# Which products of queries and keys GpSimd makes in an eight-layer sequence: three of seventeen in place of two

## The chip, the cores and the metric

The kernel runs on 1 core of one Trainium2 chip. The metric is the device time of one execution in microseconds. The engines are named as the profile names them: PE is TensorE, DVE is VectorE, ACT is ScalarE, POOL is GpSimd, and SP is SyncE, which issues the DMAs here. ("PEld" is the loading of weights into PE.)

## The reference

Four blocks of a network, each an attention-like layer and a feed-forward layer, eight layers in all, over 4 sequences of 1024 tokens with 128 features. Each layer's output is added to its input and normalised:

```python
x = L0_attn_data
x = _layernorm(x + _L0_attn_ref(x, ...), axis=-1)
x = _layernorm(x + _L0_ffn_ref(x, ...), axis=-1)
x = _layernorm(x + _L1_attn_ref(x, ...), axis=-1)
x = _layernorm(x + _L1_ffn_ref(x, ...), axis=-1)
...
```

The change lies in the third layer, an attention inside each token: every one of 16 heads has 64 scalar queries, keys and values, and the scores are all products of a query with a key up to its own index.

```python
def _L1_attn_ref(x, Wq, bq, Wk, bk, Wv, bv, Wo, bo):
    H, C = (16, 64)
    Q = (x @ Wq + bq).reshape(b, s, H, C) * inv_sqrt_c
    K = (x @ Wk + bk).reshape(b, s, H, C)
    V = (x @ Wv + bv).reshape(b, s, H, C)
    scores = jnp.einsum('bshq,bshk->bshqk', Q, K)
    mask = jnp.triu(jnp.ones((C, C), dtype=bool), 1)
    scores = jnp.where(mask, jnp.asarray(-jnp.inf, scores.dtype), scores)
    w = jax.nn.softmax(scores, axis=-1)
    attn = jnp.einsum('bshqk,bshk->bshq', w, V)
    return attn.reshape(b, s, HID) @ Wo + bo
```

So there are 4096 tokens x 16 heads x 64 queries, each against up to 64 keys, and no matrix product makes the scores: they are elementwise products.

## The kernel before

**Units.** The 4096 tokens are 32 tiles of 128, and each tile is two units of 64 tokens: 64 units. In a unit the 128 partitions are 32 tokens times 4 of the keys (key index modulo 4), and the free dimension runs over 2 lots of 32 tokens, 16 heads and the queries. The 64 keys of a head are thus 16 groups (n = 0 to 15) of 4. With a group n only the queries from 4(n + 1) on meet all its keys, so the product with "n" has 64 - 4(n + 1) queries per head (60 for n = 0, 4 for n = 14), that is 32 times as many columns. The queries on the diagonal are two more products, "d", with 32 queries per head (1024 columns) each. That makes seventeen products a unit, fed in this order (`feed`, lines 850 to 894): d1, n8 to n14, d0, n0 to n7.

**One product's way.** Each of the seventeen takes room in a ring of 8904 columns (`ringe` in the profile) and goes through the engines in turn (`rest`, from line 903 on):

1. product of queries and keys into the ring, by DVE, which reads the keys where they lie in PSUM (`ringe<-qr,kvr`), or, for the products that `SHARED` names, by POOL;
2. subtraction of the row's maximum in place, always by POOL (`ringe<-ringe,mr`);
3. exponential in place, by ACT;
4. sum over partitions into the denominators, by PE (`den`);
5. multiplication by the values in PSUM, in place, by DVE (`ringe<-ringe,kvr`);
6. sum over partitions into the numerators, by PE (`num`), after which the room in the ring is free.

Denominators, values and numerators run strictly in the order of the products. POOL can't take the keys from PSUM, so for each shared product ACT first copies the 32 keys per partition into a small tile (`ks`, in `keys_values`, lines 839 to 842).

```python
shared = (kind, i) in SHARED
yield "POOL" if shared else "DVE", self.when(
    lambda: self.ering.can(SH * nq), lambda: self.ering.back(SH * nq)
), True
...
if shared:
    self.g.tensor_tensor(e, qk[0], unit["ks"][i][:, :, None].to_broadcast(sh), ALU.mult)
else:
    self.v.tensor_tensor(e, *qk, ALU.mult)
```

**Around it.** `prepare` makes queries and the row maxima of a tile ahead (two scans, a predicated copy and a product on DVE per half), copies them with DMAs on SP's queue into `qr` and `mr`, two buffers each, and `keys_values` makes keys and values of a unit on PE into two PSUM buffers (`kvr`). `close` divides and projects a finished unit. Three further chains follow the attention through the later layers, group by group of 512 tokens (the last 512 in two groups of 256): chain a (the ternary feed-forward layer, a recurrence, an expert layer), chain b (a state space layer) and chain c (a routed layer, whose tables POOL gathers by indirect DMA: `gt<-in_f_tup`, `gt<-in_f_tdn`).

**The order.** All instructions are written out in one order per engine by a planner in the kernel (`Order`): it keeps a clock for each engine from formulas for the length of every operation (`length`), and at each step takes the task that can start first. Among tasks of one engine that could start within 0.05 us of each other it takes the most urgent kind: closing a unit, then preparing, then the three chains, then the steps 2 to 6 ("rest"), and last the products ("feed"). The feed is one sequence: the product after one on POOL is placed only when that one has been placed. At run time each engine works through its list in order and waits by semaphores.

Every operation is recorded through a helper, so all lines of the profile carry its line 60 (L60); groups are told apart by their tiles.

Of the kernel before, what the change touches and what calls it, by code (L numbers as in the profile page):

```python
# [309 lines left out]
class Model:  # L310
# [511 lines left out]
    def keys_values(self, unit, u, xt):  # L822

        for half in (1, 0):
# [13 lines left out]
            yield "ACT"  # L838
            for kind, n in SHARED:
                if n // 8 == half:  # L840
# [7 lines left out]
    def feed(self):  # L848
# [6 lines left out]
        for unit in self.units:  # L855
            seen = set()
            for kind, i in order:
# [14 lines left out]
                else:  # L872
# [5 lines left out]
                    shape = lambda tt, nq=nq: tt.rearrange("p (a q) -> p a q", q=nq)  # L878
                shared = (kind, i) in SHARED
                yield "POOL" if shared else "DVE", self.when(  # L880
# [1033 lines left out]
            self.order.run()  # L1914
        assert not self.held and all(len(self.slots[k]) >= n for k, (n, _) in self.room.items()), self.slots

SHARED = ("n", 8), ("n", 3)

URGE = {"close": 0, "prepare": 1, "chain_a": 2, "chain_b": 2, "chain_c": 2, "rest": 3, "feed": 4}
HOP = {"close": 0.2, "prepare": 0.2, "chain_a": 0.5, "chain_b": 0.5, "chain_c": 0.5, "rest": 0.1, "feed": 0.1}  # L1920
# [122 lines left out]
```

## Time and profile before

| | us |
|---|---|
| median of 3 runs | 3988.96 |
| lowest and highest run | 3988.85, 3995.15 |
| profiled execution | 3998.63 |
| its span, first to last instruction | 3996.9 |

The mean clock that PE was granted is 0.909 of full speed. Attention's products run from 88.8 us (the first on POOL) to about 3590 us; the rest of the span is the end of the three chains. The groups of the profile that belong to the steps above:

| step | engine | instructions | busy us |
|---|---|---|---|
| product | DVE | 960 | 1106.0 |
| product | POOL | 128 | 287.3 |
| subtraction | POOL | 1088 | 2549.8 |
| exponential, n | ACT | 962 (a few of other work) | 998.4 |
| exponential, d | ACT | 512 | 353.4 |
| denominators | PE | 8710 | 688.4 |
| values | DVE | 1102 (a few of other work) | 1291.3 |
| numerators | PE | 8712 | 697.7 |
| copies of keys | ACT | 128 | 22.6 |

960 + 128 products and 1088 subtractions are 64 units of seventeen. How to read the views: a group's row gives line, engine, operation, output tile <- input tiles, shapes and count, then busy time and the mean duration of one in ns, then the idle time of the engine just before them and what ended it. A row of waits gives who waited for whom, us in total, how often, and the longest.

### The profile page before, as it was taken

The numbers are of one execution on the slowest core, as the hardware profiler recorded it, in microseconds if no ns is written. First come the engines' busy times: TensorE is split into PE (matmuls) and PEld (weight loads), VectorE is DVE, ScalarE is ACT, GpSimd is POOL, SyncE is SP. The second block draws the span as 40 slices with busy tenths as digits, with TensorE's granted clock in tenths as the row PEclk, the third lists the DMA queues.
The fourth block names the chain that finished last, engine by engine and source line by source line (L and its number), as shares of the span: only waits on it lengthen the run. The fifth ranks groups of instructions, "written<-read, shape, count | busy, mean of one in ns | idle before, by whom it ended". The sixth has DMA issues, their size and how long they took to land.

```text
span 3996.9 us, 94513 instructions
## 1 busy us (share of the span) xinstructions
PE 3255.3 (81%) x38498; PEld 1703.2 (43%) x38498; DVE 3263.9 (82%) x4477; ACT 2613.7 (65%) x4970; POOL 2914.4 (73%) x1320
## 2 busy tenths in 40 slices
PE   6677677777898887888898988988898887879873
PEld 3242233333344443444354454444344443447552
DVE  3879898998988899999988889899988889983421
ACT  5675575567677786677567876677666785656441
POOL 1879996899688889698778777698787887880000
PEclk8897888888999999999899999999899998999896
DMA  3211221212223233343233234243332334522564
GB/s 86 63 46 44 56 63 44 56 43 49 57 68 93 58 93 93 76 114 88 74 95 80 70 83 105 66 128 78 96 90 63 87 80 117 148 76 70 149 147 103
DMA packets 385164, 329.13 MB, mean 82 GB/s; under 512 B 196108, under 2 KB 320460, under 8 KB 384728
## 3 DMA queue, kind: packets, MB, share of 16 engines
q1 hardware_dynamic: 375384, 289.53, 29.4%
q0 software_dynamic: 9344, 33.56, 2.8%
q8 instruction: 302, 4.95, 0.5%
q14 instruction: 134, 1.10, 0.1%
HBM read 147.85 MB, written 40.89 MB: 47 GB/s over the span
## 4 chain that ended last, share of the span: by engine, by line
PE 23%; DVE 16%; ACT 9%; issue 8%; POOL 7%; DMA 5%; SPq 1%; DVEq 0%; POOLq 0%; ACTq 0%
PE bg L60 13%; DVE ringe L60 10%; POOL ringe L60 7%; PE num L60 4%; PE den L60 4%; ACT ringe L60 4%; DVE bg L60 3%; PE kvr L60 2%; ACT b L60 1%; SPq L60 1%; ACT ha L60 1%; ACT L60 1%; DVE b L60 0%; DMA mr<-td 0%; DMA td<-gt 0%
## 5 line engine op out<-in xcount | busy, mean ns | idle before, releaser
L60 POOL TENSOR_TENSOR ringe<-ringe,mr 128x1024 f32<-128x1024 f32 (+14 forms) x1088 | 2549.8, 2378 | 524.9 <-DVE ringe L60 370.9
L60 DVE TENSOR_TENSOR ringe<-ringe,kvr 128x1024 f32<-128x1024 f32 (+14 forms) x1102 | 1291.3, 1204 | 171.0 <-PE den L60 148.4
L60 ACT ACTIVATE ringe<-ringe 128x896 f32<-128x896 f32 (+14 forms) x962 | 998.4, 1055 | 585.0 <-POOL ringe L60 582.8
L60 DVE TENSOR_TENSOR ringe<-qr,kvr 128x1024 f32<-128x1024 f32 (+12 forms) x960 | 1106.0, 1188 | 61.9 <-PE num L60 47.5
L60 PE MATMUL num<-ringe,cst 128*32 128x256 f32 (+7 forms) x8712 | 697.7, 412 | 242.6 <-DVE ringe L60 237.9
L60 PE MATMUL den<-ringe,cst 128*32 128x256 f32 (+7 forms) x8710 | 688.4, 417 | 201.7 <-ACT ringe L60 162.0
L60 PEld LDWEIGHTS num<-ringe,cst 128*32 128x32 f32 x8712 | 206.3, 113 | 589.4 <-DVE ringe L60 450.5
L60 PEld LDWEIGHTS den<-ringe,cst 128*32 128x32 f32 x8710 | 226.5, 114 | 517.8 <-ACT ringe L60 256.1
L60 ACT ACTIVATE ringe<-ringe,cst 128x256 f32<-128x256 f32 x512 | 353.4, 772 | 61.7 <-POOL ringe L60 61.2
L60 POOL TENSOR_TENSOR ringe<-qr,ks 128x896 f32<-128x896 f32 (+1 forms) x128 | 287.3, 2245 | 82.4 <-PE num L60 44.4
L60 PE MATMUL bg<-xT,a 128*128 128x512 f32 (+2 forms) x486 | 254.5, 636 | 15.4 <-DVE a L60 4.9
L60 PE MATMUL bg<-a,ha 128*128 128x128 f32 x1168 | 165.8, 288 | 14.3 <-ACT ha L60 14.3
L60 DVE TENSOR_TENSOR_SCAN bg<-ends,bg 128x512 f32<-128x512 bf16 x128 | 155.3, 1218 | 25.5 <-PE bg L60 23.9
L60 PE MATMUL kvr<-wkv,xT 128*32 128x256 f32 x2048 | 153.5, 423 | 24.3 <-DVE ringe L60 23.8
L60 PEld LDWEIGHTS bg<-a,ha 128*128 128x128 f32 x1168 | 147.5, 198 | 23.7 <-ACT ha L60 15.7
L60 POOL DMA_INDIRECT gt<-in_f_tup,dlumps x16 | 15.8, 987 | 185.4 <-ACT dlumps L60 136.5
L60 ACT COPY b<-bg 128x256 f32<-128x256 f32 (+2 forms) x216 | 96.3, 450 | 69.2 <-PE bg L60 67.0
L60 PE MATMUL bg<-xT,b 128*128 128x128 f32 (+1 forms) x884 | 133.8, 295 | 9.4 <-DVE b L60 2.8
L60 ACT ACTIVATE ha<-bg,cst 128x512 f32<-128x512 f32 (+1 forms) x150 | 98.2, 675 | 62.4 <-PE bg L60 62.1
L60 PEld LDWEIGHTS bg<-xT,a 128*128 128x128 f32 (+1 forms) x486 | 85.7, 201 | 118.9 <-issue 59.2
L60 PEld LDWEIGHTS bg<-xT,b 128*128 128x128 f32 x884 | 112.6, 198 | 48.1 <-issue 23.3
L60 ACT ACTIVATE b<-cst,little 128x128 f32<-128x128 f32 x392 | 125.0, 396 | 0.0
(653 smaller groups left out, 4652.3 us busy)
## 6 DMA issues: line engine op xcount, KB each, us to landing
qr<-q SPq DMA_DIRECT2D x512, 128.0 KB
mr<-t SPq DMA_DIRECT2D x512, 128.0 KB
a<-in_f_W SPq DMA_DIRECT2D x67, 256.0 KB
c<-in_f_Wdn SPq DMA_DIRECT2D x58, 256.0 KB
c<-tu SPq DMA_DIRECT2D x212, 64.0 KB
tu<-gt SPq DMA_DIRECT2D x26, 512.0 KB
td<-gt SPq DMA_DIRECT2D x24, 512.0 KB
c<-td SPq DMA_DIRECT2D x88, 128.0 KB
```

The source lines that it names most:

```text
L60: return f(*args, **kw)
```

## The change

`SHARED` names the products that POOL makes. Before: n8 (28 queries per head, 896 columns) and n3 (48 queries, 1536 columns), 76 queries in all. After: n10 (20 queries, 640 columns), n1 (56 queries, 1792 columns) and n5 (40 queries, 1280 columns), 116 in all. The products n8 and n3 are then made by DVE from the keys in PSUM. ACT copies three sets of keys in place of two: one in the half with n8 to n15, two in the other. The places of POOL's products among the seventeen are the 2nd and 13th before, and the 4th, 11th and 15th after.

```diff
@@ -1914,7 +1914,7 @@
-SHARED = ("n", 8), ("n", 3)
+SHARED = ("n", 10), ("n", 1), ("n", 5)
```

Nothing else differs in the text; the planner derives the order of all engines anew from it.

## The prediction

> **What bounds the kernel now.** I read the summary of engines first, then the busy time by stretch, then the groups by shape, then the waits, and last cut the stretch of attention into slices of 10 us.
>
> The busy times, with the share of the span, and the head of the chain that ended last:
>
> ```profile
> PE 3255.3 (81%) x38498; PEld 1703.2 (43%) x38498; DVE 3263.9 (82%) x4477; ACT 2613.7 (65%) x4970; POOL 2914.4 (73%) x1320
> ...
> PE 23%; DVE 16%; ACT 9%; issue 8%; POOL 7%; DMA 5%; SPq 1%; DVEq 0%; POOLq 0%; ACTq 0%
> ```
>
> No engine is full and the chain passes over all of them (as far back as it can be followed, to about 1260 us), so no single total decides. By stretch (length, then busy us and instructions of PE, weight loads, DVE, ACT and POOL, then clock and DMA):
>
> ```profile
> 100.00:3600.00 3500.00, 2905.06 (x33732) 1452.80 (x33733) 3117.43 (x4032) 2388.90 (x4316) 2880.51 (x1279) 0.92 0.31 78
> 3600.00:3997.00 397.00, 287.85 (x4537) 214.40 (x4535) 113.06 (x369) 171.10 (x521) 22.74 (x25) 0.84 0.47 117
> ...
> 400.00:600.00 200.00, 141.24 (x1449) 54.15 (x1450) 180.91 (x188) 129.82 (x180) 194.34 (x86) 0.83 0.25 59
> ...
> 1800.00:2000.00 200.00, 170.93 (x2239) 85.40 (x2243) 184.16 (x234) 135.53 (x232) 156.32 (x67) 0.92 0.32 82
> ```
>
> The changed work ends at about 3600 us; the last 397 us hold none of it. In the 3500 us before, DVE is 89.1% busy (3117.43 / 3500) and POOL 82.3%. POOL is at 97% from 400 to 600 us, DVE ahead of it at 92% to 78% from 1800 to 2000: the bound changes hands. The waits (us in total, times, longest):
>
> ```profile
> ACT ringe L60 <- POOL ringe L60: 644.0, 434, 7.2
> ...
> POOL ringe L60 <- DVE ringe L60: 378.5, 115, 34.0
> ...
> DVE ringe L60 <- PE den L60: 157.9, 136, 8.9
> ```
>
> POOL waits for products of DVE (378.5 us): DVE is late there. The exponentials wait for subtractions of POOL (644.0 us), and DVE waits for denominators, which stand behind those exponentials: POOL is late there. To weigh the two I counted, over 350 slices of 10 us from 100 to 3600 us, which engine was busy over 95%. Two such slices:
>
> ```profile
> 400.00:410.00 10.00, 8.23 (x72) 2.06 (x72) 6.95 (x6) 5.32 (x6) 10.00 (x5) 0.70 0.57 127
> 1470.00:1480.00 10.00, 7.75 (x142) 4.02 (x144) 9.89 (x17) 9.87 (x24) 6.74 (x4) 1.00 0.16 52
> ```
>
> The first counts for POOL alone, the second for DVE alone. The count: DVE alone 112 slices, POOL alone 104, both 70, neither but PE 29, none of the three 35. Up to 1000 us it is POOL 39 to DVE 20, from 1000 to 2000 us 22 to 39, from 2000 us on 43 to 53.
>
> **The change part by part.** A unit has 544 query columns per head over its seventeen products, so 17,408 columns; 64 units run. The rows for the sizes concerned (busy us, mean ns of one; then idle time):
>
> ```profile
> L60 POOL TENSOR_TENSOR ringe<-qr,ks 128x1536 f32<-128x1536 f32 x64 | 177.5, 2773 | 55.2 <-PE num L60 44.4 <-DVE ringe L60 7.7 <-ACT anm L60 2.6
> ...
> L60 POOL TENSOR_TENSOR ringe<-qr,ks 128x896 f32<-128x896 f32 x64 | 109.8, 1716 | 27.2 <-ACT ks L60 22.3 <-ACT b L60 3.4 <-DMA qr<-q 1.2
> ...
> L60 DVE TENSOR_TENSOR ringe<-qr,kvr 128x1792 f32<-128x1792 f32 x64 | 128.8, 2012 | 5.3 <-PE num L60 5.3
> ...
> L60 DVE TENSOR_TENSOR ringe<-ringe,kvr 128x1536 f32<-128x1536 f32 x64 | 111.8, 1747 | 24.0 <-PE den L60 21.9 <-ACT xT L60 2.0
> ...
> L60 DVE TENSOR_TENSOR ringe<-qr,kvr 128x1280 f32<-128x1280 f32 x64 | 94.7, 1480 | 4.4 <-PE num L60 4.3
> ...
> L60 DVE TENSOR_TENSOR ringe<-ringe,kvr 128x896 f32<-128x896 f32 x64 | 69.2, 1081 | 5.6 <-PE den L60 5.5 <-issue 0.2
> ...
> L60 DVE TENSOR_TENSOR ringe<-qr,kvr 128x640 f32<-128x640 f32 x64 | 52.2, 816 | 0.0
> ```
>
> DVE loses the products of 1792, 1280 and 640 columns: 2012 + 1480 + 816 = 4308 ns a unit. It gets back those of 1536 and 896 columns. Their rows on DVE don't exist as products; the multiplication by the values has the same shape and one operand in PSUM too, and where both rows exist they agree (1215 and 1215 ns at 1024 columns), so 1747 + 1081 = 2828 ns. DVE is relieved of 1.48 us a unit, 94.7 us in all.
>
> POOL loses 2773 + 1716 = 4489 ns a unit. Its products at 640, 1280 and 1792 columns aren't in the trace. A line through its two rows has 1.652 ns a column ((2773 - 1716) / 640) and 236 ns fixed: 1293 + 2350 + 3196 = 6839 ns, so 2.35 us more a unit, 150.4 us in all. The bounds are the two rows taken as plain rates for 3712 columns: 1.805 ns gives 6701 (2.21 us more), 1.915 ns gives 7109 (2.62 us more). I take the line: 1280 columns lie between its points, and 640 and 1792 lie 256 columns outside on either side, so that an error of its slope nearly cancels.
>
> The Trainium skill ("GPSIMD Engine Reference", section 3.1) measures GpSimd 1.96 times slower than VectorE on two-input elementwise work and keeps VectorE as the rule. Here the ratio is smaller, 1716 / 1081 = 1.59. By the page the three products would take 1.96 x 4308 = 8444 ns and the addition would be an estimated 3.96 us a unit, which makes the sum below +80 us in place of +29. The skill ("Perfetto Trace Analysis", "Optimizing Scalar/DVE Operations") also warns that the two engines share a port, so that moving work between them may not help. No such blocking shows: DVE's products run from 270 to 2158 ns over all sizes while its largest size has a mean of 2147 ns, with POOL busy 82% of the time.
>
> ACT makes three copies of keys (176 ns each) in place of two: 64 x 0.176 = 11.3 us. It is 68% busy (2388.90 / 3500), and two of the three now stand back to back behind one wait, so I cost this at nothing; uncovered it is 11.3 us. No transfer is added. The products still read the landed queries and hold the same ring space.
>
> The moved product stands in POOL's queue with the subtractions and the gathers of the last layer. It takes its place in the order in which products are fed, so nothing behind it in that order is fed first: POOL has three such points in a unit, after which DVE's next products follow. What is late behind a product on POOL is a subtraction, then its exponential on ACT, then denominators on PE, then DVE's multiplication by values. A gather can be late by at most one product (3.2 us, where it was 2.8); those after 3600 us meet none.
>
> **The sum.** POOL's work on a unit is (2549.8 + 287.3) / 64 = 44.33 us, and grows by 2.35 us, 5.3%. DVE is busy 3117.43 / 64 = 48.7 us a unit, and falls by 1.48 us, 3.0%. Where POOL alone is full, time follows POOL: 1040 us x 5.3% = +55. Where DVE alone is full: 1120 us x 3.0% = -34. Where both are full I take half of each, since either can be last: 700 us x 1.15% = +8. Where neither is full: nothing. Sum: +29 us. With the bounds of POOL's price (5.0 to 5.9%) it is +25 to +36.
>
> The profiled execution took 3998.63 us for a span of 3996.9, so the sum gives a span of 4026. This execution stands 9.7 us above the median of the runs, 3988.96; from that median the forecast is 4018 us, and the times below start from it too.
>
> **The rivals.**
>
> *DVE sets the pace (faster).* POOL is idle 620 of the 3500 us, 378.5 of them waiting for DVE. If the added 2.35 us falls into that idle time, only DVE's relief counts: -34 us where DVE alone is full, -55 with the slices where both are (1820 us x 3.0%); 3934 to 3955 us, and 3944 in the middle. For it: DVE is the busier engine, and the ring's 8904 columns hold half a unit, so that POOL can work off its backlog. Against it: the gain needs DVE-full time 1.75 times the POOL-full time (5.3 / 3.04), and it is 112 to 104. Its place is the start of a unit, where POOL waits for the first product; it decides if POOL's backlog never reaches the exponentials.
>
> *Neither engine decides (same).* PE is 83% busy and has the largest share of the chain; the gains and losses cancel within 8 us: 3981 to 3997 us. For it: 64 slices with neither of the two full. Against it: 286 with one of them or both.
>
> *POOL becomes the bound (much slower).* If the slices where both are full go POOL's way and DVE's relief is worth nothing, (1040 + 700) x 5.3% = +92 us, 4081 us; if every unit pays, +150 us, 4139 us. For it: after the change POOL carries 3031 us (2880.51 + 150.4) and DVE 3023 in the same stretch. Against it: POOL's idle time must take none of it.
>
> That the change does something else than it says is excluded: the list of shared products is read in two places only, for the copies and for the engine.
>
> **How the numbers follow.** A measurement here tells no less than about 0.2% (8 us) from no change. Forecast, slower by 8 to 92 us (3997 to 4081): 0.48. Beyond it, POOL as the bound: 0.06. Same: 0.10. Faster: 0.36, of which 0.07 beyond 3940 us, since every later decision of the order moves with the first and that can add to either side. So slower 0.54, same 0.10, faster 0.36. The range 3940 to 4080 leaves out 0.07 below and about 0.06 above; the likeliest case has 3997 to 4081.
>
> **What would show it.** POOL's three products at 1.29, 2.35 and 3.2 us and DVE's busy time down by 95 us would confirm the prices; POOL's busy time should rise to about 3065 us. The theory is right if the slices with POOL alone full grow at DVE's cost, if exponentials wait longer for POOL than 644 us, and if the first 1000 us, where POOL leads 39 to 20, lose most (+17 by the same sum: 390 x 5.3% - 200 x 3.0% + 200 x 1.15%). It is wrong if POOL's wait for DVE falls from 378.5 us by more than 100 us while the end of attention comes earlier than 3600 us: then the idle time took the work. It is wrong too if the time changes mostly after attention, in the last 397 us.

## The result, and the profile after

The changed kernel takes 4003.56 us (median of 9 runs, 3997.64 to 4012.14); before, on the same chips, 3990.8 us (9 runs, 3988.85 to 3998.6). The ratio is 1.0029, 95% interval 1.0017 to 1.0041: slower by 7 to 16 us, where +29 was forecast. The two profiled executions hide this: the one of before lies 7.8 us above its median and the one of after 2.5 us below, so that their spans, 3996.9 and 3999.3 us, differ by only 2.4 us. The traces are read below for where work moved, and the medians for what it cost.

The summary of engines after, and the head of the chain:

```profile
PE 3237.4 (81%) x38498; PEld 1690.0 (42%) x38498; DVE 3181.3 (80%) x4413; ACT 2612.4 (65%) x5034; POOL 3060.1 (77%) x1384
...
PE 34%; DVE 24%; POOL 15%; ACT 14%; issue 9%; DMA 3%; SPq 1%; DVEq 0%; POOLq 0%; ACTq 0%
```

The two stretches after (length, then busy us and instructions of PE, weight loads, DVE, ACT and POOL, then clock and DMA):

```profile
100.00:3600.00 3500.00, 2888.20 (x33609) 1435.02 (x33601) 3022.15 (x3932) 2386.37 (x4365) 3024.49 (x1341) 0.93 0.31 77
3600.00:3999.00 399.00, 287.30 (x4661) 220.32 (x4660) 128.71 (x408) 171.51 (x533) 25.59 (x28) 0.84 0.50 129
```

POOL rose from 2880.51 to 3024.49 us and DVE fell from 3117.43 to 3022.15: the two are level. The products after, by shape, on POOL and then on DVE (busy us, mean ns; idle time before them):

```profile
L60 POOL TENSOR_TENSOR ringe<-qr,ks 128x1792 f32<-128x1792 f32 x64 | 205.0, 3203 | 9.1 <-PE num L60 9.0
...
L60 POOL TENSOR_TENSOR ringe<-qr,ks 128x1280 f32<-128x1280 f32 x64 | 150.2, 2346 | 8.2 <-PE num L60 7.3 <-DVE bg L60 0.8
...
L60 POOL TENSOR_TENSOR ringe<-qr,ks 128x640 f32<-128x640 f32 x64 | 81.6, 1276 | 0.5 <-PE num L60 0.5
```

```profile
L60 DVE TENSOR_TENSOR ringe<-qr,kvr 128x1536 f32<-128x1536 f32 x64 | 111.6, 1744 | 13.2 <-PE num L60 13.1
...
L60 DVE TENSOR_TENSOR ringe<-qr,kvr 128x896 f32<-128x896 f32 x64 | 68.9, 1076 | 0.0
```

The prices of single instructions were right to within 2% (forecast 3196, 2350, 1293, 1747 and 1081 ns). The waits after (us, times, longest):

```profile
ACT ringe L60 <- POOL ringe L60: 670.6, 442, 11.0
...
POOL ringe L60 <- DVE ringe L60: 327.8, 79, 24.1
...
DVE ringe L60 <- PE den L60: 224.7, 154, 9.2
```

POOL waits less for DVE (378.5 us before), the exponentials wait a little more for POOL, and DVE, which has less to do, waits more for the denominators behind those exponentials (157.9 before). The count of 10 us slices turned the same way: POOL alone full 153 (104 before), DVE alone 83 (112), both 62 (70).

When a unit ends can be read from one instruction: the division that closes it. In order of time, the division of unit 32 in the traces of before and of after (start, length):

```profile
1786.46 0.69 DVE L60 TENSOR_TENSOR rd<-num,rd 128x512 f32<-128x512 f32 x1
```

```profile
1834.38 0.68 DVE L60 TENSOR_TENSOR rd<-num,rd 128x512 f32<-128x512 f32 x1
```

By the 32nd unit of 64 the changed kernel is 48 us late; at the 64th it is 7 us late. This shape, a loss in the first half and a gain in the second, was the first question for the experiments. The ends of units (us):

| profiled kernel | unit 16 | unit 32 | unit 48 | unit 64 | span |
|---|---|---|---|---|---|
| before | 918 | 1787 | 2709 | 3603 | 3996.9 |
| after | 949 | 1835 | 2731 | 3610 | 3999.3 |
| pair, then three | 916 | 1786 | 2701 | 3585 | 3987.3 |
| three, then pair | 949 | 1833 | 2735 | 3616 | 4015.4 |
| more on POOL, old order | 940 | 1829 | 2776 | 3702 | 4094.2 |
| less on DVE, old order | 911 | 1776 | 2696 | 3585 | 3981.1 |
| more on POOL, own order | 942 | 1844 | 2766 | 3660 | 4036.0 |
| less on DVE, own order | 912 | 1777 | 2651 | 3547 | 3940.8 |

### The profile page after: what moved, and what is told of

It is laid out like the page before. It is cut to its first block, busy times and chain, and to the rows that moved or that the text cites. A ratio compares the mean times of both kernels' runs of the same rounds, so it can differ in the third digit from the quotient of the medians.

```text
span 3999.3 us, 94470 instructions
## 1 busy us (share of the span) xinstructions
PE 3237.4 (81%) x38498; PEld 1690.0 (42%) x38498; DVE 3181.3 (80%) x4413; ACT 2612.4 (65%) x5034; POOL 3060.1 (77%) x1384
## 4 chain that ended last, share of the span: by engine, by line
PE 34%; DVE 24%; POOL 15%; ACT 14%; issue 9%; DMA 3%; SPq 1%; DVEq 0%; POOLq 0%; ACTq 0%
PE bg L60 19%; DVE ringe L60 16%; POOL ringe L60 14%; PE den L60 6%; ACT ringe L60 6%; PE num L60 6%; DVE bg L60 5%; PE kvr L60 3%; ACT ha L60 1%; ACT b L60 1%; ACT L60 1%; DVE a L60 1%; ACT bg L60 1%; ACT x L60 1%; SPq L60 1%
## 5 line engine op out<-in xcount | busy, mean ns | idle before, releaser
L60 ACT ACTIVATE ringe<-ringe 128x640 f32<-128x640 f32 (+14 forms) x964 | 998.5, 1056 | 602.0 <-POOL ringe L60 598.1
L60 DVE TENSOR_TENSOR ringe<-qr,kvr 128x1024 f32<-128x1024 f32 (+11 forms) x896 | 1011.1, 1163 | 59.9 <-PE num L60 45.0
L60 POOL TENSOR_TENSOR ringe<-qr,ks 128x640 f32<-128x640 f32 (+2 forms) x192 | 436.8, 2275 | 17.9 <-PE num L60 16.8
L60 ACT COPY b<-bg 128x512 f32<-128x512 f32 (+2 forms) x229 | 101.8, 453 | 85.4 <-PE bg L60 82.8
L60 PE MATMUL bg<-b,cst 128*128 128x512 f32 x208 | 116.6, 644 | 6.8 <-ACT b L60 5.1
```

The source lines that it names most:

```text
L60: return f(*args, **kw)
```

## The experiments

Each was timed beside the kernel before on its chip; ratios are to that, with their 95% interval. "The pair" is n8 and n3, "the three" are n10, n1 and n5.

**Halves.** The obvious reading of the table's first two rows is that POOL sets the pace of the first half and DVE that of the second. Two kernels share by the number of the unit:

```diff
-                shared = (kind, i) in SHARED
+                shared = (kind, i) in shared_of(2 * unit["T"] + unit["u"])
...
+def shared_of(k):
+    return PAIR if k < 32 else THREE
```

The copies of keys use the same function; the second kernel has the two exchanged.

> The first 32 units share as before (n8, n3), the last 32 as after (n10, n1, n5). Theory A (POOL sets the pace of the first half, where every unit pays for POOL's added 2.35 us; DVE sets it in the second half, where its relief of 1.48 us a unit comes through): unit 32 ends as before (1787 us), the second half is some 40 us shorter, and the whole takes 3945 to 3965 us against 3991, faster by 0.7 to 1.2%. Rival B (the second half of the changed kernel only catches up work of the later layers that was put off in the first half, with no gain of its own): 3985 to 4000 us. Rival C (the end hangs on the later layers, not on attention): attention ends some 40 us earlier but the whole gains less than 10 us.

> The first 32 units share as after (n10, n1, n5), the last 32 as before. Theory A: unit 32 ends 40 to 48 us later than before and nothing is got back: 4030 to 4040 us. Rival B (catching up of put-off work): the second half wins the time back with the old pair too, 3990 to 4010 us.

Measured: 3990.82 us, 0.9991 (0.9982 to 1.0000), and 4017.59 us, 1.0061 (1.0047 to 1.0074). Theory A falls: with the three in the second half alone the gain is some 4 us and not 40. Rival B is right about the first kernel and misses the second, which took more than its 3990 to 4010 us and less than theory A's 4030 to 4040. With the pair in the second half the time won back is still large: 46 us late at unit 32, 13 at unit 64. So most of this recovery needed no relief of DVE. The later layers show what could have been exchanged. The state space layer clears its state before its third group; the clearing in the trace of before, then of after:

```profile
1781.51 0.27 DVE L60 MEMSET state<- 128x256 f32 x1
```

```profile
1764.80 0.27 DVE L60 MEMSET state<- 128x256 f32 x1
```

It came 17 us earlier after, and the last of the recurrence's scans for the third group began 39 us earlier (at 1579 us, 1618 before), at a time when attention was over 40 us late. For the fourth group it was the other way round: the last scan came 49 us later (2032 us, 1983 before), while attention caught up from 48 to 22 us. A lag of attention could thus in part be a loan: what attention doesn't use of DVE and PE the later layers use, and the other way round. That is not shown. In the pair with the tolerance of 0.06 us (the last runs below) the last scan of the third group came 54 us earlier than before, at 1565 us, with unit 32 only 5 us late; so early scans don't need a late attention. (By the medians about 24 us of the 46 stayed in the second kernel.)

**The two prices on the old order.** To price POOL's addition and DVE's relief apart, two kernels keep the planner's order of before, since the planner is told of nothing:

```diff
         self.g.tensor_tensor(e, e, m, ALU.subtract)
+        if kind == "n" and nq == 40:
+            self.nc.gpsimd.tensor_tensor(e, e, self.ones[:, :SH, None].to_broadcast([P, SH, nq]), ALU.mult)
```

```diff
-        self.v.tensor_tensor(e, e, vv, ALU.mult)
+        if kind == "n" and nq == 60:
+            self.order.note("DVE", "tensor_tensor", (e, e, vv, ALU.mult), {})
+            self.nc.vector.tensor_tensor(e[:, :, :16], e[:, :, :16], vv[:, :, :16], ALU.mult)
+        else:
+            self.v.tensor_tensor(e, e, vv, ALU.mult)
```

> The order of before, with one more instruction a unit on POOL that the planner doesn't know of: the scores of n5 are multiplied by one, 1280 columns, 2.35 us, as much as the change adds to POOL. DVE's work is unchanged. Theory A: the first 32 units lose 1.2 to 2.35 us each (40 to 75 us), the last 32 less than half of that: 4040 to 4080 us in all. Rival D (POOL's idle time takes the added work): less than 15 us over before. The forecast's slices gave 5.3% of 1040 to 1740 us, +55 to +92.

> The order of before, with DVE relieved of 1.47 us a unit: the multiplication by the values of n0 covers 16 of its 60 queries per head, so the numerators of the other 44 are left without their values. POOL's work is unchanged. Theory A: nearly nothing in the first 32 units, 25 to 45 us in the last 32: 3945 to 3965 us. Rival E (a fixed order hardly lets a shorter instruction help, the changed kernel gained by its new order): faster by less than 10 us. The forecast's slices gave -34 to -55 us.

Measured: more on POOL 4099.74 us, 1.0262 (1.0248 to 1.0276), +105 us; less on DVE 3979.41 us, 0.9959 (0.9945 to 0.9972), -16 us. The added instruction has the price of the change's addition, as its row on POOL in the first kernel shows:

```profile
L919 POOL TENSOR_TENSOR ringe<-ringe,ones 128x1280 f32<-128x1280 f32 x64 | 149.7, 2339 | 5.0
```

The waits of the first kernel:

```profile
ACT ringe L60 <- POOL ringe L60: 607.1, 416, 7.2
...
ACT ringe L60 <- POOL ringe L919: 172.6, 59, 6.4
```

59 exponentials wait for the new instruction, 172.6 us in all, on top of nearly all the waiting of before (644.0 us). Of POOL's 150 us 105 arrive in the time, 1.6 us a unit and in both halves: 41 us in the first, 58 in the second (table). So POOL's lateness isn't confined to the first half, where theory A had it, and on this fixed order the second half wins nothing back. Theory A, rival D and the forecast's slices all asked for less than the 105 us. DVE's 94 us give 16, and POOL's wait for DVE hardly falls (369.4 us, 378.5 before). Rival E is nearest about DVE, though it asked for less than 10 us. The sum of the two, +89 us, is far from the change's +12, which points to the new order. (The two instructions are stand-ins: they sit at other steps than the moved products, and ACT's third copy of keys isn't in them.)

**The same two prices, with the order made for them.** The only change is that the planner records the two instructions (`self.g` and `self.v` in place of the engines themselves; the shortened one alone is recorded).

> As the run that gave POOL 2.35 us more a unit on the order of before (+105 us), but now the planner knows of the added instruction and makes the order with it. DVE's work is unchanged. Theory F (the change's cost on POOL is mostly taken back because the planner moves other work into POOL's lateness): 4005 to 4040 us. Rival G (it can't be taken back, and what saved the change was DVE's relief in a new order): 4070 to 4110 us.

> As the run that relieved DVE of 1.47 us a unit on the order of before (-16 us), but now the planner knows of the shorter instruction. The numerators of 44 of the 60 queries of n0 are again left without their values. POOL's work is unchanged. Theory F: DVE's relief is worth little in a new order too, 3965 to 3985 us. Rival G: 3900 to 3930 us.

Measured: 4037.27 us, 1.0101 (1.0086 to 1.0117), +42 us on POOL's side; 3943.39 us, 0.9869 (0.9854 to 0.9884), -52 us on DVE's. Both theories were half right: the planner takes back some 63 of POOL's 105 us, and it makes DVE's 16 us into 52. The waits with more on POOL, own order:

```profile
ACT ringe L60 <- POOL ringe L60: 675.4, 456, 10.4
...
POOL ringe L60 <- DVE ringe L60: 353.5, 90, 19.6
...
DVE ringe L60 <- PE den L60: 206.6, 148, 6.5
```

and with less on DVE, own order:

```profile
ACT ringe L60 <- POOL ringe L60: 619.8, 481, 8.0
...
POOL ringe L60 <- DVE ringe L60: 305.7, 94, 28.9
...
DVE ringe L60 <- PE den L60: 196.5, 153, 4.2
```

The exponentials' wait for POOL falls from 779.7 us (607.1 + 172.6) to 675.4 once the planner knows of the work. With less on DVE it is POOL's wait for products that falls, from 369.4 to 305.7 us. By the table the two prices now fall into different halves: POOL's addition is 57 us late at unit 32 and no later at unit 64, DVE's relief is 10 us ahead at unit 32 and 56 at unit 64. That is theory A's picture, which the two kernels of halves didn't bear out. The two prices add up to -10 us, the change measured +12. Each price is read from a single order, and is no surer than what another order of the same work moves (6 to 18 us in the last runs below).

**Places and numbers of products.** A pair of 76 queries at other places leaves the totals of both engines as before.

```diff
-SHARED = ("n", 8), ("n", 3)
+SHARED = ("n", 10), ("n", 1)
```

The others of this kind differ in that line alone: n3 by itself, n9 with n2, n11 with n0, and two further sets of three with the change's 116 queries.

> POOL makes n10 and n1: 20 + 56 = 76 queries, exactly as many as n8 and n3 have, at the changed kernel's places, without its third product n5. POOL's and DVE's totals are those of before. If the places matter (rival H: evenly spread products are what offsets the cost of the third), faster than before by 15 to 60 us. If only the totals matter (theory F), within 10 us of before.

> POOL makes n3 alone, 48 queries: POOL has 1.72 us a unit less than before, DVE 1.08 us more. By the fixed order's rates (0.70 us of time for a us of POOL, 0.17 for one of DVE) it would be 64 x (0.17 x 1.08 - 0.70 x 1.72) = -65 us, 3928 us. By theory F the planner had already taken most of POOL's cost back, so that little is left to gain: 3975 to 4000 us. If DVE is the bound when POOL has less (the rival of the forecast): 4005 to 4040 us.

> The pair of before and n5 as a third product: 116 queries, as many as in the changed kernel, so the same totals on POOL and DVE, with two of the three at the old places. Theory J (two parts: POOL's added work costs about 42 us and DVE's relief gives about 52 in an order made for it, so a third product alone is worth -10 to +5 us; the rest of the change is the exchange of n8 and n3 for n10 and n1, +10): 3980 to 4000 us. Rival K (the totals alone decide, whatever the places): as the changed kernel, 4004 to 4010 us.

> POOL makes n9 and n2: 24 + 52 = 76 queries, the totals of before at other places (3rd and 12th). It shows how far a mere exchange moves the time. Theory J: 0 to 15 us from before, either way (n10 and n1 gave +10). If a place has a cost of its own by a rule, it lies between before and n10 with n1: 3995 to 4005 us.

> POOL makes n11 and n0: 16 + 60 = 76 queries, the totals of before at the 5th and 10th place. Theory J: within 15 us of before, either way. If the cost grows with the size of the larger product, or with its nearness to the start of the second half: 4008 to 4030 us.

> POOL makes n9, n2 and n5: 116 queries at the 3rd, 12th and 15th place. With n9 and n2 alone beside it, it is a second measure of what the third product is worth: theory J -10 to +5 us against that pair; rival L (the third product costs POOL's 42 us nearly whole, and n10 with n1 hid it by chance): +25 us or more against that pair.

| products on POOL | queries | median us | ratio (95%) |
|---|---|---|---|
| n3 | 48 | 4000.77 | 1.0014 (1.0005 to 1.0023) |
| n8, n3 (before) | 76 | 3990.8 to 3996.57 | 1 |
| n9, n2 | 76 | 3977.89 | 0.9951 (0.9936 to 0.9965) |
| n10, n1 | 76 | 4006.93 | 1.0024 (1.0015 to 1.0033) |
| n11, n0 | 76 | 4065.0 | 1.0164 (1.0149 to 1.0179) |
| n8, n3, n5 | 116 | 3981.89 | 0.9963 (0.9949 to 0.9976) |
| n9, n2, n5 | 116 | 3982.37 | 0.9963 (0.9950 to 0.9975) |
| n10, n1, n5 (after) | 116 | 4003.56 | 1.0029 (1.0017 to 1.0041) |

Three pairs each stand beside the same pair with n5. The third product is worth -0.37% beside n8 and n3, +0.12% beside n9 and n2 (0.9963 less 0.9951), +0.05% beside n10 and n1: -15, +5 and +2 us, of which the last two are within their intervals. That is near theory J (-10 to +5), and against K (the totals alone) and L (POOL's cost nearly whole). On the first order the change splits in two: n10 and n1 in place of n8 and n3, +0.24%, and n5 added, +0.05%. The exchange, which moves no work between engines, made the kernel slower, where rival H had it faster by 15 to 60 us; the third product was about free. The expectations for n3 alone all missed: neither the fixed order's -65 us nor theory F's 3975 to 4000 us (just) nor a bound on DVE of +10 us or more came, but +6 us.

n9 with n2 has the lowest median of all that compute the whole result, 14 to 26 us below before by its interval, where theory J allowed 15 either way; n8, n3, n5 and n9, n2, n5 are within 5 us of it. n11 with n0 missed its expectation by far. Its trace says where attention waits, not why the planner arrives there. The rows of POOL's subtractions for n4 (1408 columns) and n5 (1280), for n11 with n0:

```profile
L60 POOL TENSOR_TENSOR ringe<-ringe,mr 128x1408 f32<-128x1408 f32 x64 | 205.0, 3203 | 89.2 <-DVE ringe L60 81.4 <-ACT ha L60 5.2 <-DVE epr L60 1.7
...
L60 POOL TENSOR_TENSOR ringe<-ringe,mr 128x1280 f32<-128x1280 f32 x64 | 187.1, 2923 | 105.5 <-DVE ringe L60 85.9 <-PE num L60 13.9 <-PE bg L60 3.1
```

and for n9 with n2:

```profile
L60 POOL TENSOR_TENSOR ringe<-ringe,mr 128x1408 f32<-128x1408 f32 x64 | 204.6, 3197 | 58.2 <-DVE ringe L60 34.4 <-PE bg L60 11.2 <-ACT b L60 8.1
...
L60 POOL TENSOR_TENSOR ringe<-ringe,mr 128x1280 f32<-128x1280 f32 x64 | 187.3, 2926 | 31.3 <-PE bg L60 27.6 <-ACT ha L60 1.6 <-DVE ringe L60 1.2
```

With n11 and n0, POOL stands idle 195 us (89.2 + 105.5) ahead of these two, 167 of them waiting for DVE, against 90 with n9 and n2, 36 of them for DVE. A reason could be that after n0 POOL has no further product of its own to fill the time until DVE delivers; no run tests that, nor whether it makes the +68 us.

**An order alone.** The last four runs change only the planner's tolerance for ties, to 0.04 and to 0.06 us, once in the kernel before and once in the changed one:

```diff
-EPS = 0.05
+EPS = 0.04
```

> The sharing of before, with the planner's tolerance for ties at 0.04 us in place of 0.05: another order of the same instructions. Theory M (an order moves the time by chance as much as the exchange of products did): 10 us or more from before, either way. Rival N (the order moves little, the places have a price): within 4 us of before.

> The sharing of after (n10, n1, n5) with the tolerance at 0.04 us. Theory M: 10 us or more from the changed kernel (1.0029 of before), either way, and against the pair at the same tolerance anything from -30 to +30 us. Rival N: 1.001 to 1.005 of before, and 8 to 16 us above the pair at the same tolerance.

> The sharing of before with the tolerance at 0.06 us. Theory M: 10 us or more from before, either way. Rival N: within 4 us of before.

> The sharing of after with the tolerance at 0.06 us. Theory M: 10 us or more from the changed kernel, either way. Rival N: 1.001 to 1.005 of before, and 8 to 16 us above the pair at the same tolerance.

| tolerance (us) | pair n8, n3 | three n10, n1, n5 | three against pair |
|---|---|---|---|
| 0.05 | 1 | 1.0029 (1.0017 to 1.0041) | +0.29% |
| 0.04 | 0.9984 (0.9975 to 0.9993) | 0.9990 (0.9981 to 0.9999) | +0.06% |
| 0.06 | 0.9973 (0.9963 to 0.9984) | 0.9984 (0.9975 to 0.9993) | +0.11% |

Another order of the very same instructions moves the pair by 6 and 11 us and the three by some 16 and 18 us. Theory M asked for 10 us in each; three of the four have it, and none stayed in rival N's ranges. So the +10 us of n10 with n1 needs no reason in their places. The +68 us of n11 with n0 is several times what an order alone did here. On all three orders the three are slower than the pair, by +0.15% on the mean (6 us); at 0.06 us the median of the three, 3987.96 us, lies above the highest run of the pair, 3985.38; at 0.04 the medians are 3 us apart, within the spread of the runs.

The pair at 0.04 us also shows which waits tell of the change. It has the work of before, and yet its exponentials wait for POOL as long as those of the changed kernel:

```profile
ACT ringe L60 <- POOL ringe L60: 670.6, 451, 10.7
...
DVE ringe L60 <- PE den L60: 147.3, 130, 5.7
```

DVE's wait for denominators is the firmer sign: 142 to 167 us in the six kernels that compute the whole result with a pair and no added work, 207 to 246 in the five with three products throughout. The ends of units are another. How far the three end behind the pair that stands beside them (us; minus is ahead):

| three against pair | unit 16 | unit 32 | unit 64 |
|---|---|---|---|
| after against before | 32 | 48 | 7 |
| the same, tolerance 0.04 | 27 | 20 | -15 |
| the same, tolerance 0.06 | 29 | 10 | 4 |
| n8, n3, n5 against n8, n3 | 34 | 46 | -5 |
| n9, n2, n5 against n9, n2 | 19 | 12 | 23 |
| n10, n1, n5 against n10, n1 | 21 | 13 | -8 |

On all six the three are late by 19 to 34 us after the first quarter of attention, and no such loss is left at the end of attention on five. What happens at unit 32 depends on the order: of the 48 us after the change, the exchange to n10 and n1 alone makes 35, and the pair at 0.04 us is 23 us behind before there and 11 ahead at unit 64. So the loss in the first half and the gain in the second are in part a matter of the one order that before happens to have.

## Why the prediction was wrong

**The prices.** Right: POOL's busy time grew to 3060.1 us (forecast about 3065), DVE's products fell from 1106.0 to 1011.1 us, 94.9 (forecast 94.7). The copies of keys on ACT cost nothing that shows: ACT is busy 2612.4 us, 2613.7 before. By section 3.1 of the "GPSIMD Engine Reference" of the Trainium skill, which has GpSimd 1.96 times slower, the forecast would have been an estimated +80 us; the measured ratio at 1280 columns is 2346 / 1480 = 1.59. The shared port of the Trainium skill's "Perfetto Trace Analysis" ("Optimizing Scalar/DVE Operations") doesn't show in these durations after either: DVE's products of 1024 columns took 1215 ns before and 1211 after, with POOL busier. (The sum's upper end with POOL's bounds is about +37 us, not +36.)

**The bound that changes hands.** Right in kind. Both engines' work reaches the time, with opposite signs. All the signs named in advance came: more slices with POOL alone full at DVE's cost, a longer wait of the exponentials (670.6 against 644.0 us), POOL's wait for DVE down by 51 us and not by 100, attention late first of all in the first 1000 us. Not each of them is proof: the wait of 670.6 us came in the pair at 0.04 us too. The early loss is the firmest, 19 to 34 us at unit 16 in six comparisons, where the same sum gave +17.

**The step that failed** is the size of one term: "Where POOL alone is full, time follows POOL: 1040 us x 5.3% = +55", with POOL's part of the slices where both are full (700 us x 5.3% / 2 = +19), +74 us in all. Measured in an order made for it, POOL's addition costs 42 us. On a fixed order the rule missed the other way: 105 us arrived. That the new order gives back 63 us is measured, on one order each; why it does stays open. The loan read from the traces (later layers run while POOL holds attention up) doesn't fit this very run: with more on POOL in its own order unit 32 is 57 us late, and so is unit 64. DVE's term (-34 and -11, -45 in all) measured -52, against -16 on a fixed order. So +74 - 45 = +29 should have been about +42 - 52 = -10 us, within what an order alone moves. The third product added to three pairs (-15, +5 and +2 us) agrees with that. With that term set right the sum is still no nearer to the measured +12; the rest is the order.

**What was not in the sum** is the order. The text named it ("every later decision of the order moves with the first and that can add to either side") and gave it no size. On the first order it is the largest part of the measured +12: n10 with n1 on the totals of before is +10 us, and the tolerance alone moves either kernel by 6 to 18 us. The sign of the forecast held at all three tolerances, but not for the reason given: POOL's price was not above DVE's, and the third product by itself was worth -15 to +5 us. As far as the two prices go, the sign was luck.

**The rivals.** "DVE sets the pace" asked that POOL's idle time take the work: 45 of 150 us didn't reach the time on a fixed order and 108 in a new one, so not all was taken. "Neither decides" had the wrong mechanism, since each of the two terms is clear of noise alone, and was nearest in size: they about cancel. "POOL becomes the bound" (+92 to +150) has the size of what POOL's addition alone cost on the fixed order, +105.

Open stays why a new order gives back so much of POOL's cost, why n11 with n0 is so much slower, and whether n9 with n2 keeps its lead under other tolerances.

## What to carry to other kernels

Counting the slices in which an engine is full did not price these instructions: POOL's addition was put at 74 us and cost 105 on a fixed order and 42 in a new one, DVE's relief was put at 45 and gave 16 and 52. Where a planner orders everything anew, price the two sides of a moved operation by one run each with the planner told of it, and one with it kept ignorant. Before reading a change of a few tenths of a per cent as an effect, make another order of the same instructions (here by a tie tolerance) and see how far that alone moves the time. A moved set of operations should be split into the exchange that leaves the totals alone and the rest: here, on the first order, the exchange made most of the loss.

## What the runs showed that was not expected

A relief of 94 us on the busiest engine (DVE, 89% in its stretch) gave 16 us while the order stood, and an addition of 150 us on a less busy one (POOL, 82%) cost 105: the share of busy time ranked the two the wrong way round for a fixed order.

GpSimd's multiplication with one operand repeated along the row cost 1.67 ns a column between 640 and 1792 columns ((3203 - 1276) / 1152), its subtraction of two full operands 2.13 ((4013 - 1556) / 1152), in the same trace.

Of the nine runs after, the three in which PE was granted a clock of 0.911 took 4009.5 to 4012.1 us and the three at 0.914 or 0.917 from 3997.6 to 4001.1. Not every kernel shows this: of the eleven runs of the three at the tolerance of 0.04 us the fastest, 3982.74 us, was at 0.911 and one of 3992.9 us at 0.913. What ties the time to the clock wasn't tested.
